# Three more entries get their products with Wa and adj ahead of their turn

## The chip, the cores and the metric

The kernel runs on one core of a Trainium2 chip. The metric is device time in microseconds, as the median of several runs; smaller is better. Five engines work side by side, each on its own list of instructions and in that list's order: PE (TensorE, products of matrices; its weight loads are shown apart as PEld), DVE (VectorE), ACT (ScalarE), POOL (GpSimd, which here issues the gathers and scatters) and SP (SyncE, which issues most plain transfers). They wait for each other by semaphores.

## The reference

32 entries of 512 nodes with 256 features go through four layers. Layers 0 and 3 are the same computation with other weights, cut here to what matters:

```python
pre_u = h @ W1[:d];  pre_v = h @ W1[d:]
S   = sigmoid(relu(pre_u[u] + pre_v[v] + b1) @ W2 + b2)     # for every pair (u, v)
a_t = (S * adj).T @ h
m_t = (adj.T @ h) * h
z   = beta1 * h + beta2 * (a_t @ Wa + ba) + beta3 * (m_t @ Wm + bm)
```

`adj` is 512 x 512 and mostly zero, so S is needed only where adj is not. Layer 1 is `z + relu((adj @ z) @ W.T + b)`. Layer 2 is an attention: a softmax over `leaky_relu(f1[i] + f1[j]) + adj`, applied to features.

Of layer 0, two parts need neither S nor any edge: `h @ Wa` (the kernel multiplies with Wa first, then with S) and `(adj.T @ h) * h`.

## The kernel before, in words

The kernel counts the entries of adj and takes a sparse path when they fit. There the 32 entries are worked off in eight groups of four (NB = 4); the time in which a group passes its middle stage is called a turn. For each group there are five streams of work, Python generators that issue a piece of work each time they are asked:

- `first` (L806): loads x of an entry, transposes it to hT, writes hT to memory as xT, and forms pre_u and pre_v, which SP writes to a table in memory (L604). Its products are L578 (transposes), L592 and L594.
- `edges` for layer 0: for each of 36 items (rows of nonzeros of adj) POOL gathers 128 rows of the table (L646), DVE adds the other side's rows (L731) and takes relu and W2 (L739 with sums on ACT at L717, or L747 with sums of its own), sigmoids follow (L614 to L675), and POOL scatters the results to cells (L639).
- `middle`: loads the cells as SA (L772), and for each of the four entries (`middle_one`, L876) ends layer 0, does layers 1 and 2, and forms pre_u and pre_v of layer 3.
- `edges` for layer 3, as above.
- `last` (L1094): ends layer 3 in the way the middle stage ends layer 0; its products with S are L1061.

In `middle_one` the order on PE is: mhT = (adj.T @ h) * h (`mhT`, L794, products at L46, DVE at L801); the product of hWa with S as laid out in `flat` (L891, ACT at L860); mhT with Wm (L898); layer 1 with zW (L912) and adjT (L46 with adjT); layer 2 with the features (L934), a transpose of their last column f (L950), a softmax on ACT and DVE (L958 to L964), the put-back of its rows by transposes (L1003, ACT at L1004), the product with eT (L46), then pre_u and pre_v (L592, L594) and transposes of the result (L992). hWa of the next entry (`hWa`, L782, products at L46 with Wa, ACT at L791) is made between the put-backs. z is formed in the tile of hT: ACT scales hT by beta1 (L896) and DVE adds the sums (L899). So each entry loads hT anew (L871, tile `hT1`, one buffer), and x into `h1` (L867) where it has to make mhT.

The first group is different: `middle_before` (L824) makes hWa and mhT of its four entries before the first turn begins, into four `big` tiles, which share their buffers (tag SA3, four of them) with the SA tiles of layer 3. The middle stage then uses these (`given`) and loads no x.

The order is written out by `weave` (L454). Each piece of each stream has a time, in units of a turn; all pieces are sorted by it. The first turn's middle stage goes from 0 to 0.53, the second's from 0.53 to 1.53, and so on. Within a stage `middle_shares` divides the time among the pieces by estimated costs, and the pieces of the edges fall between the pieces of the middle stage by these times. A stream with a list of costs (`first`, `last`) is fill: a due piece is held until a piece of the middle stage tells of room on PE (its yield's value: 0.9 after the features, 7.0 and 3.4 in the softmax, some 1.7 elsewhere) and is then issued behind that piece's last PE instruction. The framework's scheduler may bring an instruction forward in its engine's list where its inputs and its tile allow; `behind` and `issue_after` bar it from going ahead of the middle stage.

In the first turn no fill is due: the first stages of groups 0 and 1 are done before it, the first stage of group 2 is due from 0.71 to 0.97, and the last stage of group 0 from 1.09 to 1.69.

Of the kernel before, what the change touches and what calls it, by code (L numbers as in the profile page):

```python
# [8 lines left out]
F32 = mybir.dt.float32  # L9
# [7 lines left out]
P = 128  # L17
N = 512
D = 256
NC = N // P  # L20
DC = D // P
G = 32
NB = 4
# [25 lines left out]
class Model:  # L49


    def __init__(self, ctx, tc, a):
        nc = self.nc = tc.nc
        self.tc, self.a = tc, a
        const = self.const = ctx.enter_context(tc.tile_pool(name="const", bufs=1))
        self.ident = const.tile([P, P], F32, name="ident")
        make_identity(nc, self.ident)
        self.adj = const.tile([P, NC, N], F32, name="adj")
        for c in range(NC):
            nc.sync.dma_start(self.adj[:, c, :], a["adj"][c * P : (c + 1) * P, :])  # L60
        self.g0, self.g3 = self.gnn_first("L0_gnn"), self.gnn_first("L3_gnn")
# [361 lines left out]
class Sparse:  # L423
# [3 lines left out]
    def __init__(self, ctx, m, counts, xr, outr, B):  # L427
        self.m, self.nc, self.tc, self.counts = m, m.nc, m.tc, counts
        tc = m.tc
        self.xr, self.outr = xr, outr  # L430
        pool = lambda n, b, **k: ctx.enter_context(tc.tile_pool(name=n, bufs=b, **k))
        self.dram = pool("dram", 1, space=bass.MemoryType.DRAM)

        self.cells = {
            k: [self.dram.tile([CELLS + SPARE, NB], F32, name=f"cells_{k}{q}") for q in range(2)] for k in "03"
        }
        self.lists = self.dram.tile([N, 2 * N], F32, name="lists")
        self.x2s = self.dram.tile([B, P, NC, D], F32, name="x2s")

        self.xT, self.x2T = (self.dram.tile([B, P, DC, N], F32, name=n) for n in ("xT", "x2T"))  # L440
        self.e = Edges(m, pool("edges", 1))
        self.adjT = pool("adjT1", 1).tile([P, NC, N], F32, name="adjT")
        self.grp = pool("grp", 2)
        self.act, self.small, self.gath = pool("act", 1), pool("small", 2), pool("gath", 5)
        self.ps = pool("ps", 7, space=PSUM)
        self.ps_f1 = pool("ps_f1", 1, space=PSUM)
        self.later, self.bigs, self.given, self.marks = None, 0, None, {}
        self.main = None
        self.before = {(k, q): [] for k in "03" for q in range(2)}

# [352 lines left out]

    def first(self, g, i):  # L806


        def load(b):
            h = self.act.tile([P, NC, D], F32, name="h0", tag="h", bufs=2)  # L810
            self.nc.sync.dma_start(h, self.xr[i + b])
            return h

        h = load(0)
        for b in range(NB):
            ahead = load(b + 1) if b < NB - 1 else None
            hT = self.turned(h, "hT0", "hT")
            yield
            self.nc.scalar.dma_start(self.xT[i + b], hT)
            yield from self.pre(g, b, hT)  # L820
            h = ahead
        self.settle()

    def middle_before(self, g0, i):  # L824

        self.given = []
        for b in range(NB):
            h, hT = self.fresh(i + b)
            hT = hT()
            both = self.big(F32, 2048, 3).rearrange("p (k n) -> p k n", k=2)  # L830
            hWa = both[:, 0, :].rearrange("p (c d) -> p c d", c=NC)
            mhT = both[:, 1, :].rearrange("p (c n) -> p c n", c=DC)
            for _ in self.hWa(g0, hT, 0, hWa):
                yield
            for _ in self.mhT(h, hT, 0, mhT):
                yield
            self.given.append((hWa, mhT))

    def middle(self, g0, g3, i):


        SA = self.load(g0, 0)
        given, self.given = self.given, None
        h, hT = self.fresh(i, given)
        hT = hT()
        hWa = None
        if not given:
            for hWa in self.hWa(g0, hT, 0):
                yield
        flat = self.flat(SA, 0)  # L850
        for b in range(NB):
            keep = [h, hT, hWa, flat]
            yield from self.middle_one(g0, g3, b, i + b, SA, keep, given)
            h, hT, hWa, flat = keep
        self.settle()
# [20 lines left out]
    def middle_one(self, g0, g3, b, i, SA, keep, given):  # L876
        nc, m, w = self.nc, self.m, g0.w
        act, small, psum = self.act, self.small, self.psum
        h, hT, hWa, flat = keep
        if given:  # L880
            hWa, mhT = given[b]
        else:
            for mhT in self.mhT(h, hT, 0):
                yield
# [15 lines left out]
            yield 4.0 * (c == DC - 1)  # L900
        more = b < NB - 1
        if more:
            keep[0], turned = self.fresh(i + 1, given)

        zW = act.tile([P, NC, D], F32, name="zW", tag="hWa0")
        halves = [(0, psum()), (2, psum())]
# [20 lines left out]
        eT = act.tile([P, NC, N], F32, name="eT")  # L927
        if more:
            keep[1] = turned()
            ahead = None if given else self.hWa(g0, keep[1], 0)  # L930
        pns = [psum() for _ in range(NC)]
        for r in range(DC):
            for ic, pn in enumerate(pns):
# [4 lines left out]
                    start=(r == 0),  # L938
# [182 lines left out]
def even(n):  # L1121
    return [1.0] * n
# [2 lines left out]

FIRST, LAST, AHEAD = even(NB * 5 + 1), even(NB * 8 + 1), even(NB * 4 + 1)
ENDS, BEHIND = even(NB * 6 + 1), even(NB * 2 + 1)


def spread(shares, a, b):  # L1130

    times, at = [], 0.0
    for share in shares:
        times.append(a + (b - a) * at / sum(shares))
        at += share
    return times
# [6 lines left out]
    return first + spread(even(ITEMS), a, b) + spread(even(TAIL), b, behind)  # L1143


def middle_shares(given):


    hWa = [] if given else [1.7, 1.7]
    shares = list(hWa)  # L1150
    for b in range(NB):
        more = hWa if b < NB - 1 else []
        shares += [] if given else [2.8, 2.8]
        shares += [3.4, 3.4, 1.0, 2.7]
        shares += [1.7, 3.4, 2.8, 4.5] + [0.9] * NC
        shares += [0.4, 0.4, 0.4, 1.0, 0.4, 1.0] + more + [1.5, 1.5]
        shares += [2.8, 4.5] + [0.4] * NC + [0.5, 0.5]
    return shares + [0.1]


@with_exitstack
def sparse_path(ctx, m, counts, xr, outr, B):


    sp = Sparse(ctx, m, counts, xr, outr, B)
    last = B // NB - 1
    streams = [
        (sp.setup(), spread(even(NC + 1 + NC + 2 * (OWN // 2 + 1) + 1), -0.40, -0.295), ""),
        (sp.setup_behind(), spread(even(2 * (OWN // 2 + 1) + 2 * PANELS + 4), -0.285, -0.16), ""),
        (sp.setup_rest(), spread(even(7), -0.26, -0.20), ""),  # L1170
        (sp.zeros_behind(), spread(even(2), 0.15, 0.2), ""),
    ]
    for t in range(last + 1):
        g0, g3 = Group(sp, m.g0, f"0_{t}"), Group(sp, m.g3, f"3_{t}")
        start, end = (max(0.0, k - 0.47) for k in (t, t + 1))

        if t == 0:
            first = spread(FIRST, -0.385, -0.30)
            edges0 = edge_times(-0.292, -0.27, -0.03, -0.02, LEAD_AT_ENDS)
        elif t == 1:  # L1180
            first = spread(FIRST, -0.28, -0.06)
            edges0 = edge_times(0.02, 0.07, start - 0.06, start - 0.04)
        else:
            first = spread(FIRST, start - 0.82, start - 0.56)
            edges0 = edge_times(start - 0.552, start - 0.505, start - 0.06, start - 0.04)
        edges3 = edge_times(end + 0.003, end + 0.05, end + 0.48, end + 0.54)
        behind = end + 0.56, end + 1.16
        if t == last - 1:
            edges3 = edge_times(end + 0.003, end + 0.05, end + 0.46, end + 0.5)
            behind = end + 0.7, end + 1.06  # L1190
        if t == last:
            end -= 0.2
            edges3 = edge_times(end + 0.003, end + 0.02, end + 0.45, end + 0.46, LEAD_AT_ENDS)
            behind = end + 0.29, end + 0.45
        streams += [
            (sp.first(g0, t * NB), first, FIRST_US),
            (sp.edges(g0, ("yT", "mhT0", "hWa0") if t == 0 else ()), edges0, ""),
            (sp.middle(g0, g3, t * NB), spread(middle_shares(t == 0), start, end), "main"),
            (
                sp.edges(g3, *((("yT", "h1", "hT1"), ("mhT0", "hWa0")) if t == last else ())),  # L1200
                edges3,
                "free",
            ),
        ]
        if t == 0:
            streams.append((sp.middle_before(g0, 0), spread(AHEAD, -0.15, -0.03), ""))
        if t < last:
            streams.append((sp.last(g3, t * NB), spread(LAST, *behind), LAST_US))
        else:
            streams.append((sp.last_before(g3, t * NB), spread(ENDS, *behind), ""))  # L1210
            streams.append((sp.last_behind(g3, t * NB), spread(BEHIND, end + 0.5, end + 0.6), ""))
    sp.weave(streams)
# [237 lines left out]
```

## Time and profile before

| what | value |
|---|---|
| median of 3 runs | 2996.85 us |
| the runs | 2991.82 to 2997.82 us |
| the profiled execution | 2998.45 us |
| its span | 2996.8 us |
| busy: PE, DVE, POOL, ACT | 90%, 77%, 52%, 45% |
| setup, first stages, first edges | 0 to 245 us |
| first turn (four entries given) | 245 to 475 us |
| second turn | 475 to 814 us |
| third turn | 814 to 1155 us |

In a line of a timeline the columns are start, length, engine, line, operation, tiles written and read, shape, count, and in brackets how long the engine had been idle and what ended that. A line of a table of windows has the window, its length, the busy time of PE, PEld, DVE, ACT and POOL (with the number of instructions), the granted clock of PE, the share of the DMA engines and GB/s. A product of 512 columns takes about 0.43 us of PE at full clock (16 of them pass in 6.87), though the mean of one is given as 592 ns, since they overlap.

### The profile page before, as it was taken

The numbers are of one execution on the slowest core, as the hardware profiler recorded it, in microseconds if no ns is written. First come the engines' busy times: TensorE is split into PE (matmuls) and PEld (weight loads), VectorE is DVE, ScalarE is ACT, GpSimd is POOL, SyncE is SP. The second block draws the span as 40 slices with busy tenths as digits, with TensorE's granted clock in tenths as the row PEclk, the third lists the DMA queues.
The fourth block names the chain that finished last, engine by engine and source line by source line (L and its number), as shares of the span: only waits on it lengthen the run. The fifth ranks groups of instructions, "written<-read, shape, count | busy, mean of one in ns | idle before, by whom it ended". The sixth has DMA issues, their size and how long they took to land. (4 is left out here: it accounts for less than half of the span.)

```text
span 2996.8 us, 32453 instructions
## 1 busy us (share of the span) xinstructions
PE 2690.0 (90%) x8645; PEld 1613.9 (54%) x8646; DVE 2307.1 (77%) x6035; ACT 1336.8 (45%) x4101; POOL 1555.3 (52%) x1328
## 2 busy tenths in 40 slices
PE   6367787989998999989999899989999899988998
PEld 3134344545664566546664466646565466644666
DVE  6874786889588885988778885888858896783494
ACT  3553454445344443544344443445434453453262
POOL 2662463646445673556536464466735564361183
PEclk9678998999999999999999999999999999999999
DMA  8875657796678867787677866687677866663474
GB/s 268 286 225 169 213 174 221 233 300 203 217 217 269 268 211 227 230 262 254 209 222 247 275 207 230 216 268 253 211 228 236 303 227 197 208 211 102 148 244 150
DMA packets 302143, 677.30 MB, mean 226 GB/s; under 512 B 52608, under 2 KB 170880, under 8 KB 293760
## 3 DMA queue, kind: packets, MB, share of 16 engines
q0 software_dynamic: 122688, 414.40, 42.9%
q1 hardware_dynamic: 160304, 223.52, 23.0%
q10 hardware_dynamic: 18960, 37.24, 3.4%
q8 instruction: 70, 1.15, 0.2%
q14 instruction: 121, 0.99, 0.1%
HBM read 529.02 MB, written 146.01 MB: 225 GB/s over the span
## 5 line engine op out<-in xcount | busy, mean ns | idle before, releaser
L646 POOL DMA_INDIRECT rows<-table,iv x552 | 679.0, 1230 | 795.5 <-DMA table<-puv 262.7
L639 POOL DMA_INDIRECT cells<-s,cell x576 | 697.6, 1211 | 420.6 <-DVE s L675 243.2
L731 DVE TENSOR_TENSOR rows<-rows,mine 128x1024 f32<-128x1024 f32 x552 | 666.4, 1215 | 101.4 <-DMA rows<-table,iv 72.8
L717 ACT ACTIVATE rows<-rows 128x256 f32<-128x256 f32 x1088 | 439.6, 406 | 445.4 <-DVE rows L739 396.6
L46 PE MATMUL pst<-adj,h 128*128 128x512 f32 x1024 | 452.2, 592 | 0.0
L747 DVE SCALAR_TENSOR_TENSOR rows<-rows,L_gnn_W2bc 128x256 f32<-128x256 f32 x1120 | 414.0, 417 | 1.6
L739 DVE SCALAR_TENSOR_TENSOR rows<-rows,L_gnn_W2bc 128x1024 f32<-128x1024 f32 x272 | 329.4, 1213 | 0.4
L46 PEld LDWEIGHTS pst<-adj,h 128*128 128x128 f32 x1024 | 192.8, 190 | 219.9 <-issue 217.6
L46 PE MATMUL pst<-L_gnn_Wa,hT 128*128 128x256 f32 x1024 | 248.8, 393 | 62.9 <-DMA hT<-xT 57.8
L46 PEld LDWEIGHTS pst<-L_gnn_Wa,hT 128*128 128x128 f32 x1024 | 198.9, 199 | 103.0 <-issue 59.2
L46 PE MATMUL pst<-eT,feats 128*128 128x512 f32 x512 | 237.7, 619 | 10.9 <-ACT eT L1004 10.9
L46 PE MATMUL pst<-adjT,zW 128*128 128x512 f32 x512 | 228.2, 599 | 11.6 <-ACT zW L916 9.7
L596 DVE TENSOR_TENSOR puv<-pst,bc_L_gnn_b 128x256 f32<-128x256 f32 x256 | 104.9, 416 | 162.4 <-DMA table<-puv 89.2
L597 ACT COPY puv<-pst 128x256 f32<-128x256 f32 x256 | 93.2, 371 | 288.1 <-DVE puv L596 225.9
L1061 PE MATMUL pst<-hWa,SA 128*128 128x256 f32 x896 | 220.3, 400 | 0.0
L1061 PEld LDWEIGHTS pst<-hWa,SA 128*128 128x128 f32 x896 | 213.8, 328 | 3.7 <-issue 1.7
L717 ACT ACTIVATION_READ_ACCUMULATOR rows<-rows 128x1 f32 x1088 | 204.7, 188 | 0.0
L860 ACT COPY flat<-SA 128x512 f32<-128x512 f32 x128 | 136.7, 1128 | 136.6 <-issue 62.9
L891 PE MATMUL pst<-flat,hWa 128*128 128x512 f32 x448 | 196.8, 592 | 0.0
L592 PE MATMUL pst<-w_L_gnn_W,hT 128*128 128x512 f32 x256 | 141.5, 681 | 53.9 <-ACT hT L579 36.5
L46 PEld LDWEIGHTS pst<-eT,feats 128*128 128x128 f32 x512 | 99.9, 198 | 133.2 <-issue 113.3
L46 PEld LDWEIGHTS pst<-adjT,zW 128*128 128x128 f32 x512 | 96.5, 191 | 133.4 <-issue 114.0
(176 smaller groups left out, 3984.2 us busy)
## 6 DMA issues: line engine op xcount, KB each, us to landing
table<-puv SPq DMA_DIRECT2D x256, 256.0 KB
SA<-cells POOLq DMA_DIRECT2D x64, 1024.0 KB
h<-in_x_dram SPq DMA_DIRECT2D x64, 512.0 KB
mine<-table SPq DMA_DIRECT2D x64, 512.0 KB
hT<-xT SPq DMA_DIRECT2D x36, 512.0 KB
xT<-hT ACTq DMA_DIRECT2D x32, 512.0 KB
x2T<-yT SPq DMA_DIRECT2D x32, 512.0 KB
x2s<-x ACTq DMA_DIRECT2D x64, 256.0 KB
```

Source lines behind the costliest of these rows:

```text
L46: nc.tensor.matmul(out, lhsT, rhs, start=(n == 0), stop=(n == len(pairs) - 1))
L592: nc.tensor.matmul(pp, hT[:, 0, ks], w["W1"][:, 0::DC, :], start=True, stop=False)
L596: nc.vector.tensor_tensor(puv[:, 0, :], pp[:, 0:D], w["b1bc"], ALU.add)
L639: ins = self.nc.gpsimd.indirect_dma_start(out=g.cells[half], out_offset=bass.IndirectOffsetOnAxis(ap=at, axis=0), in_=s, in_offset=None)
L646: self.nc.gpsimd.indirect_dma_start(out=rows, out_offset=None, in_=g.table, in_offset=bass.IndirectOffsetOnAxis(ap=at, axis=0))
L717: self.behind(nc.scalar.activation(part, part, AF.Identity, accum_out=g.s[:, k, b : b + 1]))
L731: self.behind(nc.vector.tensor_tensor(rows, rows, other, ALU.add))
L739: nc.vector.scalar_tensor_tensor(by_entry, by_entry, 0.0, w2, ALU.max, ALU.mult)
L747: nc.vector.scalar_tensor_tensor(part, part, 0.0, w["W2bc"], ALU.max, ALU.mult, accum_out=at)
L860: self.nc.scalar.copy(flat[:, r, :], SA[r][:, :, b])
L891: nc.tensor.matmul(pz, hWa[:, r, cs], flat[:, r, :], start=(r == 0), stop=False)
L1061: self.nc.tensor.matmul(pz[:, k * D : (k + 1) * D], SA[r][:, cs, b], hWa[:, r, :], start=(r + k == 0), stop=(alone and k == 1 and r == NC ...
```

## The change

The second group's entries 0, 1 and 2 are made as the first group's are, by `middle_before`, now with a number of entries `n`. It runs as fill during the first turn: its four pieces for an entry (two halves of hWa, two of mhT) are due at 1.5, 2.5 and 3.5 entries into the first turn, at stated costs of 1.7, 1.7, 3.4 and 3.4, and the end of the generator at 4.5. Each takes the `big` tile that the first turn's entry 0, 1 or 2 has left. Here it loads x into the tile tag `h` and hT into the tag `hT`, which are those of `first` and `last`, and not into `h1` and `hT1` of the middle stage. The middle stage of the second turn uses what is given for entries 0 to 2, and makes hWa and mhT for entry 3 as before. `given` becomes a list for each group, and `middle_shares` divides a turn by the number of entries that are given.

```diff
-    def middle_before(self, g0, i):
+    def x_of(self, i):
+        h = self.act.tile([P, NC, D], F32, name="h0", tag="h", bufs=2)
+        self.nc.sync.dma_start(h, self.xr[i])
+        return h
...
+    def middle_before(self, g0, i, n=NB):
-        self.given = []
-        for b in range(NB):
-            h, hT = self.fresh(i + b)
-            hT = hT()
+        given = self.given[i] = []
+        for b in range(n):
+            if i:
+                h = self.x_of(i + b)
+                hT = self.act.tile([P, DC, N], F32, name="hT0", tag="hT")
+                self.nc.sync.dma_start(hT, self.xT[i + b])
+            else:
+                h, hT = self.fresh(i + b)
+                hT = hT()
...
-        given, self.given = self.given, None
+        given = self.given.pop(i, [])
...
-        if given:
+        if b < len(given):
             hWa, mhT = given[b]
...
-            keep[0], turned = self.fresh(i + 1, given)
+            keep[0], turned = self.fresh(i + 1, b + 1 < len(given))
...
-            ahead = None if given else self.hWa(g0, keep[1], 0)
+            ahead = None if b + 1 < len(given) else self.hWa(g0, keep[1], 0)
...
+GIVEN = {0: NB, 1: NB - 1}
+AHEAD_US = [1.7, 1.7, 3.4, 3.4]
...
+def ahead_times(end):
+    entry = end / NB
+    return [(k // 4 + 1.5) * entry for k in range(4 * GIVEN[1] + 1)]
...
-    hWa = [] if given else [1.7, 1.7]
-    shares = list(hWa)
+    hWa = [1.7, 1.7]
+    shares = [] if given else list(hWa)
     for b in range(NB):
-        more = hWa if b < NB - 1 else []
-        shares += [] if given else [2.8, 2.8]
+        more = hWa if given <= b + 1 < NB else []
+        shares += [] if b < given else [2.8, 2.8]
...
-            (sp.middle(g0, g3, t * NB), spread(middle_shares(t == 0), start, end), "main"),
+            (sp.middle(g0, g3, t * NB), spread(middle_shares(GIVEN.get(t, 0)), start, end), "main"),
...
+        if t == 1:
+            streams.append((sp.middle_before(g0, NB, GIVEN[1]), ahead_times(start), AHEAD_US))
```

More of the change, by code (lines that the diff above doesn't have):

```diff
@@ L446, in __init__ @@
         self.ps_f1 = pool("ps_f1", 1, space=PSUM)
-        self.later, self.bigs, self.given, self.marks = None, 0, None, {}
+        self.later, self.bigs, self.given, self.marks = None, 0, {}, {}
         self.main = None
@@ L802, in mhT @@
             yield mhT
+    def x_of(self, i):
+        h = self.act.tile([P, NC, D], F32, name="h0", tag="h", bufs=2)
+        self.nc.sync.dma_start(h, self.xr[i])
+        return h
     def first(self, g, i):
[L809 to L814, printed above, removed]
+        h = self.x_of(i)
         for b in range(NB):
-            ahead = load(b + 1) if b < NB - 1 else None
+            ahead = self.x_of(i + b + 1) if b < NB - 1 else None
             hT = self.turned(h, "hT0", "hT")
@@ L836, in middle_before @@
                 yield
-            self.given.append((hWa, mhT))
+            given.append((hWa, mhT))
     def middle(self, g0, g3, i):
         SA = self.load(g0, 0)
-        given, self.given = self.given, None
+        given = self.given.pop(i, [])
         h, hT = self.fresh(i, given)
```

## The prediction

> **What bounds the kernel now.** I read the shares of the engines first, then the span by stage, then PE in the first turn, and last the waits of the engines that stand beside it. The page's first part says that PE is the busiest engine over the span and DVE the next:
>
> ```profile
> PE 2690.0 (90%) x8645; PEld 1613.9 (54%) x8646; DVE 2307.1 (77%) x6035; ACT 1336.8 (45%) x4101; POOL 1555.3 (52%) x1328
> ```
>
> An average says nothing about a change that touches two of eight turns, so the next view is the busy time of each engine by entry. The first four rows are the four entries of the first turn (245 to 475 us), then a row for each entry of the second, and the last is the whole third turn. Columns: window, its length, PE, PEld, DVE, ACT, POOL, granted clock, DMA share, GB/s.
>
> ```profile
> 245.20:303.80 58.60, 48.01 (x133) 25.11 (x132) 30.00 (x74) 25.89 (x56) 6.45 (x6) 0.88 0.44 143
> 303.80:365.40 61.60, 44.52 (x134) 23.55 (x133) 45.39 (x116) 30.05 (x87) 33.04 (x32) 0.89 0.67 218
> 365.40:422.50 57.10, 47.29 (x134) 24.53 (x133) 46.22 (x120) 30.10 (x87) 31.77 (x26) 0.88 0.57 182
> 422.50:474.90 52.40, 45.79 (x135) 24.39 (x134) 34.98 (x109) 23.46 (x57) 20.62 (x20) 0.90 0.49 172
> 474.90:551.50 76.60, 65.05 (x204) 36.48 (x203) 64.48 (x168) 37.46 (x113) 40.21 (x34) 0.93 0.77 233
> 551.50:644.30 92.80, 81.00 (x240) 42.37 (x239) 79.96 (x242) 43.52 (x130) 53.78 (x44) 0.94 0.78 254
> 644.30:726.40 82.10, 77.03 (x262) 48.11 (x261) 72.18 (x181) 40.75 (x129) 53.43 (x45) 1.00 0.79 253
> 726.40:813.90 87.50, 85.78 (x286) 54.42 (x285) 61.09 (x169) 32.55 (x94) 45.28 (x39) 1.00 0.62 206
> 813.90:1155.00 341.10, 324.92 (x1060) 195.18 (x1059) 279.56 (x757) 154.06 (x462) 191.52 (x160) 0.99 0.74 239
> ```
>
> See three things. In the first turn PE is idle 44 us of 230 and the granted clock is low; nothing is full there, and the entry's own chain sets the pace. In the first two entries of the second turn PE and DVE are both near 85%, so neither alone is the bound. In its last entry PE is at 98%.
>
> Where PE is idle in the first turn stands in the timeline of PE. One softmax (transpose of f at L950, then the put-backs at L1003):
>
> ```profile
> 391.06 0.95 PE L950 MATMUL f<-ident,feats 128*128 128x128 f32 x4
> 398.28 1.09 PE L1003 MATMUL pst<-ident,ex 128*128 128x128 f32 x4 [6.28 <-DVE cols L963]
> 399.78 1.12 PE L1003 MATMUL pst<-ident,ex 128*128 128x128 f32 x4 [0.41 <-DVE ex L964]
> 401.99 1.12 PE L1003 MATMUL pst<-ident,ex 128*128 128x128 f32 x4 [1.09 <-DVE ex L964]
> 403.40 1.12 PE L1003 MATMUL pst<-ident,ex 128*128 128x128 f32 x4 [0.30 <-DVE ex L964]
> 405.25 9.71 PE L46 MATMUL pst<-eT,feats 128*128 128x512 f32 x16 [0.73 <-ACT eT L1004]
> ```
>
> And what starts the second turn: the 16 products with Wa and the 16 with adj, end to end, ahead of the first product with S (L891):
>
> ```profile
> 474.90 3.62 PE L46 MATMUL pst<-L_gnn_Wa,hT 128*128 128x256 f32 x16
> 478.35 7.03 PE L46 MATMUL pst<-adj,h 128*128 128x512 f32 x16
> 485.22 7.03 PE L891 MATMUL pst<-flat,hWa 128*128 128x512 f32 x16
> ```
>
> **The change part by part.** The sum is made against the profiled execution, 2998.45 us (span 2996.8 and 1.65 around it), which is 1.6 above the median 2996.85.
>
> *What moves.* Per entry 3.45 us of PE for hWa (474.90 to 478.35) and 6.87 for mhT (478.35 to 485.22): 10.3, and for three entries 30.9. With each go two ACT copies (0.58) and two DVE products (0.69). They leave the second turn (all 10.3 of the start; 10.3 each between the starts of entries 0 and 1 and of entries 1 and 2) and come into the softmaxes of entries 1, 2 and 3 of the first: the due time 1.5 entries lies just before that entry's feats, so the first half of hWa goes into the room of 0.9 ahead of f's transposes and the other three pieces into the room of 7.0 behind them.
>
> *First turn, what it costs.* The windows from f to the product with eT:
>
> ```profile
> 330.93:350.74 19.81, 5.12 (x21) 3.27 (x20) 15.19 (x42) 11.38 (x29) 9.97 (x9) 0.66 0.52 167
> 391.06:405.25 14.19, 5.27 (x21) 3.27 (x19) 12.19 (x35) 11.30 (x29) 6.44 (x7) 0.70 0.47 152
> 447.52:458.75 11.23, 5.17 (x21) 3.27 (x19) 7.38 (x21) 8.10 (x18) 4.91 (x7) 0.67 0.73 276
> ```
>
> In each, PE needs at least 10.3 of fill, 0.95 for f, 1.8 for the four put-backs at their quick spacing (4 x 0.44, as at 792 us) and about 1 for the last copy: 14.1. The chain itself grows by the 1.7 of the piece ahead of f, and by up to 2.5 if both DVE products and both copies fall into it. Entry 1: 19.81 covers the fill, so +2.5. Entry 2: 14.19 + 1.7, so +1.7. Entry 3: the fill is longer than the chain, 14.1 - 11.2 = +2.9. Together +7.1. Against it: the 16 products with eT took 9.71 and 8.56 behind the idle gaps of entries 2 and 3, and 7.13 in entry 1, where put-backs ran close before; with PE kept busy I take back 2.6 + 1.4 = 4.0. That leaves +3. Bounds: 30.9 if nothing is hidden, -4 if all is and the quicker products stay.
>
> [...]
>
> *Loads.* Each of the three entries loads x and xT on SP. The x loads take no new place: SP's list shows loads of x for the third turn (line L811) issued at 117.54 and 168.38 as soon as a tile was free, some 350 us ahead of their use at 524.64, and the moved entries take those places. The third turn's then wait for tiles freed at some 345, 400 and 460, still ahead of 524. New are three loads of hT (0.33 us of SP and 512 KB each; the middle stage loads hT again, since it becomes z in place). The first is issued when the first stage leaves its tile, near 220, just ahead of the loads at 227.33 and 228.06 on which PE waits 6.00 us at 233.29: +1 (0 to 3, at 1 MB in some 6 us). The other two come at about 345 and 400 behind the products before them; SP waits there with table writes and `mine` loads behind it, and SP stood 27 us at 246.14 in this trace with no engine waiting for what lay behind. 0, and up to 3 if the cover is gone. POOL: the four SA loads for layer 3 now need tiles that entries 0 to 2 of the second turn release; before, they went out from 641.18 to 659.73 and were used at 690.61. The last now waits for entry 2's product with Wm (L898, 658 before, some 635 after), behind it on POOL stand gathers. 0, up to 3.
>
> *Second turn, what it gives.* Start and entry 0 together lose 20.6 of PE, but edges of layer 3 can't start earlier: POOL's first gather waits for the last table write and goes at 481.74, rows are there at some 487. From 485.2 to 558.4, the next entry's first product, DVE is busy 65.7 of 73.2. DVE's 68.2 from 474.9 on falls by 1.4 (two products) and by 6.5: with fewer shares per entry the plan gives this one 15.7 items of edges for 18.1, each 2.7 (1.22 + 1.21, or 1.22 + 4 x 0.36, and a share of the sigmoids). Of the 60.3 left, 3.9 lie ahead of 487; 56.4 end at 543 if DVE never waits, at 550 at its 90% of before. Entry 1 starts then, not at 558.4: a gain of 9 to 15, I take 12. In entry 1 (558.4 to 651.2) PE falls from 81.0 by 10.3 and gains the 5.2 of the first stage's fill (L578, L592, L594) that no longer fits entry 0's softmax: 76 of PE, and some 75 of DVE. At 87%, as before, that is 87 us; at the 94% of entry 2, 81; I take 8 of gain (5 to 10.3). Entry 2 keeps its work. Entry 3 gets 3.9 more items of edges, 10.5 of DVE on 61 of 87.5: 1.5 back (0 to 5). Sum -18.5.
>
> *A new wait.* With mhT given, nothing but the load of hT holds ACT's scaling (L896), and it can stand in front of the softmax. That is seen in the first turn, where all four entries were given:
>
> ```profile
> 336.49 0.81 ACT L896 ACTIVATE hT<-hT,L_gnn_bcol,bc_L_gnn_beta 128x512 f32<-128x512 f32 x1 [4.99 <-DMA hT<-xT]
> 337.20 2.40 ACT L958 ACTIVATE ex<-f,fcol 128x512 f32<-128x512 f32 x4
> ```
>
> Queued behind it: the four `ex` of the softmax, and DVE and PE behind those. In the first turn's three softmaxes the gaps were about 0, 4.99 and 0.96; three more entries at that mean of 2.0 make 6, half of it covered by other work: +3 (0 to 15). [...] The row at 395.42 with 0.96 says that the load is mostly there.
>
> Sum: +3 + 1 - 18.5 + 3 = -11.5, 2987 for the profiled execution, **2985 for the median**.
>
> **The rivals.** (B) *DVE takes the bound over in the second turn.* For it: 90% in entry 0. Against it: 61 us of idle DVE in the turn. Entry 0 gives 9, entry 1 5, entry 3 takes 5, the wait on hT 6; with +4 in the first turn the change is +1 (2990 to 3002 with its bounds; 2998).
> (C) *Slower: the fill stands in front of the put-backs in PE's order and is not hidden.* Place: the three softmaxes of the first turn. Price: up to 30.9; at +26, entries 2 and 3 fully exposed and half of entry 1, the sum is 26 + 1 - 15.5 = +11.5, 3008. It decides from a cost of 20.5, where the sum passes +6. For it: the chain of entry 3 is 11.2 long and the fill 10.3, so that little disorder exposes it. Against it: 8 to 15 us of idle PE in each window, and data loaded long before.
> (D) *All of the 30.9 comes out.* First turn +1, second -30.9 + 3 for the wait: -27, 2970. Against it: the gathers that start at 481.74 whatever PE does.
> (E) *The change does nothing:* the pieces slip out of the first turn because the room is not found. They would land in the second turn, as before: 2997. The rooms of 0.9 and 7.0 in each entry speak against it.
>
> **How the numbers follow.** Two times that differ by under 0.2% (6 us) can't be told apart here: the three runs of before span 6.0. Forecast 0.48 (2975 to 2991, its own range), D 0.13, B 0.17, E 0.03, C 0.19. Faster: D, the forecast but for 0.02, and a small part of B's lower end, 0.60. Slower: C and B's end above 3003, 0.20. The rest, 0.20, is the same. The range of 8 in 10 goes from D's middle to part of C: 2968 to 3004.
>
> **What would show it.** Right: products with Wa and adj writing `big` inside 330 to 475, three runs of 16 of each; the window of entry 3 from f to eT near 14 us, entries of the first turn longer by 3 us at most, eT's 16 products near 7.1; the second turn opening with L891 and no L46 with Wa; its entries 0 and 1 some 20 us shorter together; DVE in entry 0 above 90%. Wrong: PE idle before a product that writes `big` with a DMA of hT as its releaser (C, by the loads); L1003 waiting on nothing but PE (C); ACT L896 idle for more than 5 us on hT<-xT in the second turn; later turns of another length than 341, which nothing here foresees and which would make the sum wrong by what the order of instructions alone does.

## The result and the profile after

| what | before | after |
|---|---|---|
| median | 2997.82 us | 3016.02 us |
| the runs | 2991.82 to 2999.68 us | 3010.5 to 3025.14 us |
| ratio, 95% interval | 1 | 1.007 (1.0045 to 1.0095) |
| the profiled execution | 2998.45 us | 3025.14 us (span 3023.5) |

The changed kernel is slower by 18 us where 12 us of gain were forecast; the time lies 12 us above the upper end of the range. A second comparison is among the experiments (ratio 1.0062). The profiled execution is the slowest of the five, 9 us above their median; where a second profiled execution of the same kernel (3000.2 us, from that comparison) shows something else, it stands beside the first.

Lines below the diff stand some five further down in the changed kernel: L891 is now L896, L896 is L901, L899 is L904, L950 is L955, L964 is L969 and L1003 is L1008.

The page's first part, the busy time of the engines over the span, of the kernel after:

```profile
PE 2701.3 (89%) x8645; PEld 1622.4 (54%) x8646; DVE 2308.1 (76%) x6035; ACT 1335.6 (44%) x4101; POOL 1558.4 (52%) x1328
```

The work of these engines is the same to the instruction and PE's share has fallen: 27 us of span came, of which PE is busy for 11, at a lower granted clock (0.953 for 0.959 over the span), and DVE, ACT and POOL for 3.1 or less. Where they came stands in the busy time by entry, with the same marks as in the prediction (four entries of the first turn, four of the second; window, length, PE, PEld, DVE, ACT, POOL, granted clock, DMA share, GB/s), of the kernel after:

```profile
241.80:300.90 59.10, 47.44 (x133) 25.58 (x132) 30.02 (x74) 25.73 (x56) 6.44 (x6) 0.88 0.44 140
300.90:365.20 64.30, 55.92 (x166) 29.95 (x165) 46.63 (x118) 30.98 (x89) 33.94 (x32) 0.92 0.70 229
365.20:426.60 61.40, 55.47 (x167) 29.92 (x166) 47.36 (x122) 30.79 (x89) 31.11 (x26) 0.92 0.56 182
426.60:479.80 53.20, 51.83 (x167) 28.63 (x166) 35.95 (x111) 25.78 (x61) 20.40 (x20) 1.00 0.50 179
479.80:553.90 74.10, 53.82 (x149) 28.19 (x148) 55.58 (x144) 32.89 (x99) 33.27 (x28) 0.82 0.71 214
553.90:644.80 90.90, 74.64 (x217) 38.68 (x216) 77.68 (x232) 43.35 (x136) 50.88 (x42) 0.92 0.72 233
644.80:732.30 87.50, 72.02 (x231) 45.29 (x230) 69.46 (x185) 35.91 (x115) 56.38 (x48) 0.90 0.77 246
732.30:833.10 100.80, 91.11 (x294) 56.92 (x293) 70.92 (x194) 36.30 (x107) 50.20 (x43) 0.97 0.61 198
```

| stage | before, us | after, us | difference | after, second execution | difference |
|---|---|---|---|---|---|
| first turn, entry 0 (no fill) | 58.6 | 59.1 | +0.5 | 57.8 | -0.8 |
| first turn, entries 1 to 3 | 171.1 | 178.9 | +7.8 | 179.7 | +8.6 |
| second turn, entries 0 and 1 | 169.4 | 165.0 | -4.4 | 161.6 | -7.8 |
| second turn, entries 2 and 3 | 169.6 | 188.3 | +18.7 | 182.0 | +12.4 |

The first turn began 3.4 us earlier than before (241.8 for 245.2). At the start of the third turn 19.2 us are lost, at that of the fourth 23.0 (its first product with S comes at 1191.78 for 1168.80), at the end 26.7. In the second execution 8.2 are lost at the start of the third turn and 1.7 at the end. So the 8 us of the first turn and the pattern of the second (its first half shorter, its second half longer by more) are in both; some 10 of the second turn's 14.3, and what was lost behind it, are not.

In the second turn PE's busy time fell from 308.9 to 291.6 us, and its granted clock from 0.97 to 0.91. In entry 2 PE is now busy 72 of 87.5 us; before, 77 of 82. The time came as idle time. This is what ended PE's waits there, the waits of PE over the second turn (engine, tile and line that waited, what it waited for; us in total, times, longest), of the kernel after:

```profile
PE pst L1008 <- DVE ex L969: 25.6, 8, 10.5
PE f L955 <- ACT feats L947: 7.0, 2, 6.8
PE pst L917 <- issue: 6.0, 1, 6.0
PE pst L46 <- ACT eT L1009: 5.3, 3, 2.8
```

and the head of the same view of the kernel before:

```profile
PE pst L1003 <- DVE ex L964: 8.7, 3, 7.3
PE pst L592 <- ACT hT L579: 4.5, 1, 4.5
```

The put-backs of the softmax wait 25.6 us for the DVE step before them (8.7 before): the gap that the products and the first stage's fill used to cover is open, and the step at its end comes no earlier. In the second execution they wait 22.0.

In the first turn the fill went where it was to go. PE's timeline for the softmax of its entry 2 (start, length, engine, line, operation, tiles, shape, count, idle time before and its releaser), of the kernel after:

```profile
389.73 1.89 PE L46 MATMUL pst<-L_gnn_Wa,hT 128*128 128x256 f32 x8
391.45 0.60 PE L955 MATMUL f<-ident,feats 128*128 128x128 f32 x4
391.89 1.89 PE L46 MATMUL pst<-L_gnn_Wa,hT 128*128 128x256 f32 x8
393.62 7.03 PE L46 MATMUL pst<-adj,h 128*128 128x512 f32 x16
400.48 0.60 PE L1008 MATMUL pst<-ident,ex 128*128 128x128 f32 x4
...
406.13 1.12 PE L1008 MATMUL pst<-ident,ex 128*128 128x128 f32 x4 [2.89 <-DVE ex L969]
...
409.80 9.22 PE L46 MATMUL pst<-eT,feats 128*128 128x512 f32 x16 [1.05 <-ACT eT L1009]
```

The fill runs in the gap, with no wait for a load, and ends when the first put-back is ready. But the 16 products with eT still take 9.22 us and not 7.13. The three windows from f to eT and, last, the stretch of the put-backs alone, of the kernel after:

```profile
329.67:348.47 18.80, 12.72 (x45) 7.31 (x44) 16.80 (x44) 11.75 (x29) 10.05 (x9) 0.84 0.66 209
391.45:409.80 18.35, 12.50 (x46) 7.12 (x44) 12.79 (x32) 11.53 (x29) 4.78 (x5) 0.84 0.45 152
453.29:465.07 11.78, 10.95 (x46) 6.62 (x44) 8.16 (x22) 9.87 (x20) 3.32 (x5) 1.00 0.73 290
400.50:409.80 9.30, 3.45 (x18) 2.20 (x17) 8.45 (x21) 5.33 (x17) 0.89 (x1) 0.68 0.35 113
```

Only in entry 3 does the clock stay at 1.00. In entry 2 it is 1.00 in the fill behind f (391.89 to 400.50) and 0.68 in the 9.3 us behind it, where PE is idle 5.85 us in pieces.

Entry 2's window grew most, by 4.2 us. What it waited for shows in ACT's timeline at its start, of the kernel before:

```profile
392.04 2.42 ACT L958 ACTIVATE ex<-f,fcol 128x512 f32<-128x512 f32 x4 [0.41 <-PE f L950]
395.42 0.81 ACT L896 ACTIVATE hT<-hT,L_gnn_bcol,bc_L_gnn_beta 128x512 f32<-128x512 f32 x1 [0.96 <-DMA hT<-xT]
```

and of the kernel after:

```profile
394.25 0.81 ACT L901 ACTIVATE hT<-hT,L_gnn_bcol,bc_L_gnn_beta 128x512 f32<-128x512 f32 x1 [3.96 <-DMA hT<-xT]
...
395.44 1.84 ACT L963 ACTIVATE ex<-f,fcol 128x512 f32<-128x512 f32 x3
```

ACT's scaling of the next entry's hT now stands ahead of the softmax and waits for its load, and the first `ex` starts 4.0 us behind f, for 1.0 before. All five traces with the fill have this order and a wait of 3.6 to 4.2 us there; before it was 0.96.

The wait that the prediction added to the second turn is there, twice: 3.56 us in the softmax of entry 0 (at 516.26) and 5.04 in entry 1. In entry 1, ACT's timeline of the kernel after:

```profile
595.83 0.81 ACT L901 ACTIVATE hT<-hT,L_gnn_bcol,bc_L_gnn_beta 128x512 f32<-128x512 f32 x1 [5.04 <-DMA hT<-xT]
...
598.15 0.89 ACT L947 COPY feats<-pst 128x257 f32<-128x257 f32 x3
```

The copies of the features stand behind it, and f behind them (the 6.8 in PE's waits above).

### The profile page after: what moved, and what is told of

The parts are those of the page before. It is cut to its first block, busy times and chain, and to the rows that moved or that the text cites. A ratio compares the mean times of both kernels' runs of the same rounds, so it can differ in the third digit from the quotient of the medians.

```text
span 3023.5 us, 32446 instructions
## 1 busy us (share of the span) xinstructions
PE 2701.3 (89%) x8645; PEld 1622.4 (54%) x8646; DVE 2308.1 (76%) x6035; ACT 1335.6 (44%) x4101; POOL 1558.4 (52%) x1328
## 5 line engine op out<-in xcount | busy, mean ns | idle before, releaser
L731 DVE TENSOR_TENSOR rows<-rows,mine 128x1024 f32<-128x1024 f32 x552 | 666.5, 1216 | 115.5 <-DMA rows<-table,iv 75.7
L596 DVE TENSOR_TENSOR puv<-pst,bc_L_gnn_b 128x256 f32<-128x256 f32 x256 | 104.8, 416 | 158.0 <-DMA table<-puv 73.9
L896 PE MATMUL pst<-flat,hWa 128*128 128x512 f32 x400 | 175.7, 592 | 0.0
```

Source lines behind the costliest of these rows:

```text
L596: nc.vector.tensor_tensor(puv[:, 0, :], pp[:, 0:D], w["b1bc"], ALU.add)
L731: self.behind(nc.vector.tensor_tensor(rows, rows, other, ALU.add))
L896: nc.tensor.matmul(pz, hWa[:, r, cs], flat[:, r, :], start=(r == 0), stop=False)
```

## The experiments

Three theories were stated with the first runs; their letters are not those of the prediction's rivals. **A**: the second turn is paced by DVE or by the order of the edges' instructions among the middle stage's, the products were covered there and their leaving gains nothing. **B**: the times that `middle_shares` gives to the pieces that remain do the harm, not the products. **C**: the fill itself disturbs, by its loads or tiles. Each kernel is compared with the kernel before, run beside it on the same chip; "old times" are the times that the remaining pieces had in the kernel before, "new times" those of the changed kernel.

### The change in its parts

Fill alone: made in the first turn and then left unused, while the second turn forms its products as before at the old times.

```diff
-        given = self.given.pop(i, [])
+        given = self.given.pop(i, []) if i == 0 else []
```

> The three entries are made as fill in the first turn, but the second turn doesn't use them: it makes its own products, at the times of before. 30.9 us of PE more than before, so this is the price of the fill alone. Theory A (the second turn is paced by DVE and by the order of edges in front of its softmax, and loses its cover with the products): first turn +8 as in the changed kernel, the second as before, 3003 to 3008. Theory B (the new times of the pieces do the harm): the same, since the times are those of before. Theory C (the fill itself, its loads and tiles, disturbs what follows): 3015 or more.

Measured: 1.0025 (1.0008 to 1.0042), 2983.07 for 2974.66 us, +8.4. Its first turn has the same entries 1 to 3 as the changed kernel: from the first product with S at 295.42 to the start of the second turn at 474.70 they take 179.3 us (171.1 before). The fill costs 8 us, and all of it where it stands; of C that much holds.

The products taken out, with no fill; the second turn's entries 0 to 2 read the first group's tiles instead. New times first, then old times:

```diff
-            streams.append((sp.middle_before(g0, NB, GIVEN[1]), ahead_times(start), AHEAD_US))
...
-        given = self.given.pop(i, [])
+        given = self.given.get(0, [])[: GIVEN.get(i // NB, 0)]
```

> No fill; in the second turn entries 0 to 2 use the products that the first group left in the same tiles, so they compute with another group's hWa and mhT and the output is not the reference's. 30.9 us of PE less than before, times of the pieces as in the changed kernel. The forecast of before the result: 20 us faster, 2978. Theory A: no faster than before, 2997 to 3010. Theory B: slower, like the changed kernel, some 3005 to 3012. Theory C: 2978, since no fill is there.

> The products of entries 0 to 2 are left out of the second turn (another group's are used, so the output is not the reference's), no fill, times of before, and nothing else: 30.9 us of PE less in the second turn. The forecast before the result: 20 us faster. Theory A (the chain of the middle stage through DVE, with the edges' instructions in between, sets the pace, and PE only waits longer): within 8 of before.

Measured: 1.0015 (0.9996 to 1.0035), 2981.71 for 2974.66, with new times; 1.0011 (0.9994 to 1.0027), 2986.94 for 2983.05, with old times. **30.9 us of PE work less, nothing put in its place, and no gain at all.**

The changed kernel with old times, and the kernel before with new times and nothing moved:

```diff
-            (sp.middle(g0, g3, t * NB), spread(middle_shares(GIVEN.get(t, 0)), start, end), "main"),
+            (sp.middle(g0, g3, t * NB), middle_times(there, counted, start, end), "main"),
...
+def middle_times(there, counted, start, end):
...
+    times = spread([x if c else 0.0 for x, _, c in full], start, end)
+    return [t for t, (_, k, _) in zip(times, full) if k]
```

(`full` has all pieces of a turn; a piece of an entry below `counted` gets no share of the time, one of an entry below `there` isn't issued.)

> The changed kernel, but in the second turn each piece that is left has the time that it had before the change, so that edges and fill fall between the same pieces as before. Theory B: the loss goes, 2980 to 2995. Theory A: it stays, 3008 to 3020, since PE still has less to do in front of each softmax and DVE as much. Theory C: it stays.

> The kernel before, with no product moved, but in the second turn the times of the changed kernel: the pieces that the change takes away are still there and count nothing in the plan. Theory B: slower by 10 to 20, 3007 to 3017. Theories A and C: within 6 of before, 2991 to 3003.

Measured: 1.0044 (1.0028 to 1.006), 2985.68, +11; and 1.0053 (1.0035 to 1.0071), 2988.23, +14. So new times do harm with nothing else changed, and B is a part of it but not the whole: with old times the changed kernel is still slower. The parts add up within their intervals: fill +8, taking out +4, together the +11 of the changed kernel at old times. What is left to its 1.0062 to 1.007, some 6 us, is put down to the new times by subtraction; the intervals overlap (1.0028 to 1.006 and 1.0042 to 1.0082), so this share is not shown by itself.

The changed kernel again, beside some of these:

> The changed kernel once more, beside these on one chip: 1.007 of before, as measured, 1.005 to 1.009.

Measured: 1.0062 (1.0042 to 1.0082), 3008.55 for 2991.89.

### Why less work gains nothing

The two edge streams of the second turn made empty, in the kernel before and with the products taken out:

```diff
+        if g.name in ("3_0", "0_2"):
+            for _ in range(LEAD + ITEMS + TAIL):
+                yield
+            return
```

> The kernel before, but the two streams of edges that fall into the second turn do nothing: no gathers, no DVE work, no scatters of theirs (the cells keep what an earlier group left, so the output is not the reference's). Every theory: faster, since DVE, POOL and the transfers are relieved; PE's own work is some 300 us of the turn's 339, so 20 to 40 us faster.

> The same without the two streams of edges, and without the products of entries 0 to 2 in the second turn. To be read against the run before it. Theory A: with no edges between the steps of the chain PE is the bound, and the 30.9 come out nearly whole, 20 to 31 us faster than that run. If something other than the edges holds the turn (the load of hT, the chain of the softmax alone): under 12.

Measured: 0.9931 (0.9906 to 0.9956), 2957.6 us, and 0.9826 (0.9797 to 0.9854), 2927.85 us. Without the edges, the same removal that gave nothing gives 29.75 us of the 30.9. The windows from one entry's f to the next (from the last f of the first turn; columns as above) show it entry by entry. Products taken out at old times, edges there:

```profile
445.00:509.00 64.00, 45.97 (x134) 25.26 (x133) 38.94 (x103) 26.66 (x72) 19.68 (x20) 0.87 0.70 227
509.00:590.00 81.00, 66.62 (x196) 35.93 (x195) 74.07 (x203) 43.39 (x138) 52.52 (x44) 0.89 0.75 239
590.00:692.00 102.00, 77.04 (x218) 42.45 (x217) 80.92 (x236) 40.94 (x128) 55.41 (x49) 0.85 0.82 260
```

The kernel before without the edges:

```profile
443.00:503.50 60.50, 54.48 (x167) 29.88 (x166) 17.64 (x45) 21.23 (x39) 5.46 (x7) 0.94 0.35 124
503.50:582.50 79.00, 73.57 (x228) 40.53 (x227) 28.00 (x78) 27.44 (x54) 0.00 (x0) 0.96 0.32 108
582.50:661.30 78.80, 77.84 (x248) 44.25 (x247) 28.60 (x81) 25.51 (x50) 0.00 (x0) 1.00 0.28 96
```

The same with the products taken out:

```profile
448.00:498.00 50.00, 43.40 (x134) 24.01 (x133) 16.25 (x43) 19.91 (x37) 5.38 (x8) 0.93 0.45 159
498.00:567.00 69.00, 62.95 (x197) 34.46 (x196) 26.35 (x76) 27.45 (x54) 0.54 (x1) 0.95 0.39 132
567.00:638.50 71.50, 69.46 (x215) 38.67 (x214) 27.32 (x79) 22.76 (x46) 0.54 (x1) 0.98 0.34 113
```

Without edges each stretch loses some 10 us. With them, the kernel before has 65.1, 89.7 and 92.0 in these three stretches (447.52, 512.63, 602.30 and 694.34 in its trace), together 246.8; with the products taken out they are 64.0, 81.0 and 101.8, together 246.8 as well. The stretch from entry 0's f to entry 1's gave 8.7 and the next took 9.8. The other three traces with the products gone at old times show the same two (79.2 to 82.4, then 99.6 to 101.3).

What holds the sum where it was is seen by counting one step of the edges, DVE's add of the other side's rows (L731), in DVE's timeline from the last f of the first turn on. The table gives us from that f to the add of that number (72 in the turn, 36 for each of the two layers):

| add | before | products out, old times | changed, old times | changed kernel | changed kernel, second execution | products out, new times | before, new times |
|---|---|---|---|---|---|---|---|
| 1st | 40.1 | 38.4 | 39.0 | 39.4 | 38.8 | 38.5 | 45.6 |
| 18th | 96.8 | 96.3 | 96.2 | 106.3 | 105.6 | 105.3 | 111.1 |
| 36th | 184.0 | 182.7 | 184.1 | 197.1 | 194.8 | 192.6 | 194.4 |
| 54th | 261.3 | 261.1 | 261.0 | 266.3 | 262.4 | 261.4 | 265.4 |
| 71st | 326.8 | 323.4 | 325.8 | 351.1 | 340.1 | 338.7 | 342.1 |
| 72nd | 337.9 | 334.4 | 336.9 | 354.9 | 345.0 | 342.5 | 345.9 |

With old times the edges run through the second turn at the same pace, to within 4 us in 338, whether PE has its 30.9 us of products there or not; 4 us is also what executions differ by, since the run with the fill alone, whose second turn is that of before, has 333.7 for the 72nd. Between the edges stand the steps of the middle stage, in written order. That the stage therefore goes at the edges' pace is a reading of this table, which the runs without edges support. With new times the edges fall behind in the first entries (the plan gives these fewer items), by 8 to 14 us at the 18th, and the last is still 5 to 17 late. How late does not tell what each version loses: the kernel before with new times lost 14, the changed kernel some 6 by them, and with the products out and no fill the new times cost nothing that can be told (1.0015 for 1.0011).

What DVE itself waits for in the long entry (589.9 to 691.7), the head of DVE's waits with the products taken out at old times:

```profile
DVE puv L596 <- DMA table<-puv: 12.8, 3, 6.8
DVE s L618 <- ACT s L614: 4.3, 1, 4.3
```

and in the same entry of the kernel before (602.3 to 694.3):

```profile
DVE puv L596 <- issue: 4.9, 1, 4.9
DVE puv L596 <- DMA table<-puv: 4.2, 1, 4.2
```

DVE is busy 81 of 102 us, so it is not full either: it stands at L596, which needs a tile that a table write has to free, with edges and stage steps behind it in its list. Of its three waits 5.2 us lie in the first stage and the longest, 6.8, in the middle stage's own pre_u.

The same in the changed kernel, in DVE's timeline between the products with Wm (which end on PE at 655.2) and the add that layer 1 of entry 2 needs:

```profile
655.43 1.23 DVE L731 TENSOR_TENSOR rows<-rows,mine 128x1024 f32<-128x1024 f32 x1 [1.04 <-DMA rows<-table,iv]
...
656.67 1.23 DVE L731 TENSOR_TENSOR rows<-rows,mine 128x1024 f32<-128x1024 f32 x1
...
659.27 1.22 DVE L739 SCALAR_TENSOR_TENSOR rows<-rows,L_gnn_W2bc 128x1024 f32<-128x1024 f32 x1
660.41 1.27 DVE L904 TENSOR_TENSOR hT<-hT,pst 128x512 f32<-128x512 f32 x2
```

The sum on PE is ready at 655.2; DVE takes it up at 660.41, behind two items of edges. That is PE's 6.0 us in front of L917 in its waits.

Is it the supply of the gathers? Every second gather of the two streams left out, the rows of the one before used twice:

```diff
+            if g.name in ("3_0", "0_2") and n % 2:
+                fetched[n] = self.even, t
+                return
```

> The kernel before, but in the second turn every second gather of rows is left out, and its item works on the rows of the item before (wrong sums, so the output is not the reference's); DVE and ACT do the same work as before. If the supply of gathered rows holds the edges and with them the turn: 8 to 20 us faster. If DVE's own work and its order do: within 8 of before.

Measured: 1.0004 (0.999 to 1.0017), 2981.33 for 2983.05. Half the gathers change nothing; their supply does not set the pace.

Is it DVE's busy time? DVE's add of the edges left out in the second turn (72 x 1.2 us), in the kernel before, and with the products taken out at old times:

```diff
-            self.behind(nc.vector.tensor_tensor(rows, rows, other, ALU.add))
+            if not g.name in ("3_0", "0_2"):
+                self.behind(nc.vector.tensor_tensor(rows, rows, other, ALU.add))
```

> The kernel before, but the edges that fall into the second turn (layer 3 of the first group, layer 0 of the third) leave out the addition of the other side's rows on DVE (L731, 72 of them, 1.22 us each), so their S is wrong and the output is not the reference's. DVE's busy time in the turn falls from 278 to some 190 us. Theory A (DVE and the order on it set the pace there): 10 to 25 us faster than before. If PE sets the pace: 0 to 5 faster.

> The same leaving out, and the products of entries 0 to 2 are left out of the second turn as in the run that only took them away (another group's are used), at the times of before. To be read against the run before it, which differs by the 30.9 us of PE alone. Theory A: with DVE relieved the products' 30.9 come out at last, 15 to 28 us faster than that run. If the gathers or the scaling on ACT hold the turn: within 8 of it.

Measured: 1.0178 (1.0158 to 1.0199), 3043.05 for 2991.89, 51 us slower with 87 us of DVE work less, where a gain was expected; and 1.0058 (1.0035 to 1.008), 3012.61. DVE's waits in the second turn, of the kernel before without the adds:

```profile
DVE rows L748 <- DMA rows<-table,iv: 90.3, 31, 12.3
DVE rows L740 <- DMA rows<-table,iv: 38.5, 18, 7.8
```

DVE now waits 129 us for gathered rows, with the stage's steps behind these waits (12.2 us in the kernel before for gathered rows of either side, in 9 waits). The edit changed the order as well as the work, so it does not answer the question it was made for. It shows another thing: work taken from the busy engine of an ordered list cost more here than it saved. Against this slowed base the products do come out, at 30 us, with the gathers, the scatters and the rest of the edges' work still there. So it is not the mere presence of edges that takes the gain; DVE's adds, or the order of its list with them in it, are part of it.

### The new wait, and two moves in the plan

ACT's scaling of hT held behind what stands before it in the written order, with the products taken out, and in the changed kernel, both at old times:

```diff
-            nc.scalar.activation(zT[:, c, :], hT[:, c, :], AF.Identity, bias=w["bcol"][:, c, :], scale=w["beta1"])
+            last = self.last_of(nc.scalar.engine)
+            ins = nc.scalar.activation(
+                zT[:, c, :], hT[:, c, :], AF.Identity, bias=w["bcol"][:, c, :], scale=w["beta1"]
+            )
+            if i // NB == 1:
+                order = mybir.DependencyInfo(mybir.DependencyClass.NoSync, mybir.DependencyReason.DATA)
+                self.tc.add_manual_dep(ins.ins, last, order, reason="not ahead of the softmax")
```

> The products of entries 0 to 2 are left out of the second turn (another group's are used, so the output is not the reference's), no fill, times of before, and ACT's scaling of hT (L896 of before) may not go ahead of the ACT instruction that stands before it in the program, so that it can't stand in the softmax and wait for its load. If that wait took the gain: 10 us or more faster than before. Theory A: within 6 of before.

> The changed kernel with the times of before in the second turn, and ACT's scaling of hT held behind the ACT instruction that stands before it in the program, in the second turn. Without the holding it was 1.0044. If the wait on hT is a cost of 3 to 6 us as in the run with products taken out (0.9991 against 1.0011): 1.002 to 1.0035. If it is none: 1.004 to 1.005.

Measured: 0.9991 (0.9979 to 1.0002), 2989.28 for 2991.89, against 1.0011 not held; and 1.0045 (1.0022 to 1.0067), 3008.01 for 2997.15, against 1.0044 not held. The runs not held are from other chips. The intervals overlap in the first pair and the second pair is equal. The wait on hT in the second turn is real and costs nothing that these runs can tell. The hold acts there alone; in entry 2 of the first turn ACT still waits 3.56 us.

The edge streams of the second turn 0.015 of a turn (some 5 us) later in the kernel before:

```diff
+            edges3 = edge_times(end + 0.003 + 0.015, end + 0.05 + 0.015, end + 0.48 + 0.015, end + 0.54 + 0.015)
...
+            edges0 = edge_times(start - 0.552 + 0.015, start - 0.505 + 0.015, start - 0.06 + 0.015, start - 0.04 + 0.015)
```

> The kernel before, with layer 3's edges of the first group and layer 0's of the third 0.015 of a turn later (5 us) and nothing else changed. If the place of the edges between the steps of the middle stage decides, as theory A has it: a change of 3 to 15 us, sign open. If only the amount of work does: within 3 of before.

Measured: 0.9987 (0.997 to 1.0004), 2994.75 for 2997.15. A shift as a whole costs nothing: its 18th add is 10.8 us late (107.6) and its last in time again (337.7 for 337.9). The new times cost 14 us, and there the last is 8 late. So it is not lateness in the plan alone but how the items are spread among the stage's pieces.

Other work for the first turn's gaps: the first stage of the third group due there (0.15 to 0.5) in the kernel before, with nothing else moved.

```diff
-            first = spread(FIRST, start - 0.82, start - 0.56)
+            first = spread(FIRST, start - 0.82, start - 0.56) if t > 2 else spread(FIRST, 0.15, 0.5)
```

> The kernel before, with the first stage of the third group (transposes, products with W1, their 16 x 3 DVE instructions, the table) due from 0.15 to 0.5 instead of 0.71 to 0.97: fill of 41 us of PE and some 20 us of DVE moved out of the second turn into the first. Theory A: the second turn gains what DVE loses and more, 10 to 20, the first costs 10 to 20, since each softmax there hides some 8 of 10; 0 to 10 faster in all. If PE's load alone counted: the second turn would gain 40.

Measured: 1.0031 (1.0012 to 1.0049), 3007.44 for 2997.15, +10. This does not pay either. No version that does the whole work was measurably faster than the kernel before.

## Why the prediction was wrong, by its own steps

- **What bounds the kernel.** It said of the second turn's first entries that PE and DVE are both near 85%, "so neither alone is the bound". That was a right reading of shares and stopped there: what sets the end is the stream of edges with the stage's steps between them, and it has idle time of its own. The count of the edges' adds would have shown that stream in the trace of before.
- **Second turn, -18.5: this step failed.** It took the edges' start as fixed (right: 40.1 and 39.4 us after the last f) and their pace as DVE's busy time at 90%, and let the stage go faster with fewer items and less PE work. Entry 0 came out 2.5 shorter for 12, entry 1 1.9 for 8, entry 2 5.4 longer for none, entry 3 13.3 longer for 1.5: +14.3. In the second execution it is 2.9 and 4.9 shorter, 4.8 and 7.5 longer: +4.6. At old times the removal alone costs +4 (-2 to +8), and without edges it gives 29.75. With the whole of the edges there nothing of the 30.9 comes out: the gain behind entry 0's f (8.7 at old times) was real and was given back an entry later. One reading in the sum was off without changing it: DVE's work ahead of 487 is 3.2, not 3.9.
- **The plan's new times.** "Later turns of another length than 341, which nothing here foresees" was as near as the prediction came. The forecast took the fewer items in entry 0 (15.7 for 18.1) as less DVE work there, a part of the 12 of gain. They were edges put off, and the edges are what sets the end. Measured: +14 with nothing moved, some +6 in the changed kernel by subtraction, nothing with the products out and no fill.
- **First turn, +3: right mechanism, wrong size.** Measured +7.8 in the windows and +8.4 alone. The cost of the fill, +7.1, was close: the windows from f to eT became longer by -1.0, +4.2 and +0.6, and 1.7 each goes ahead of f, +8.9 in all. Entry by entry that is +0.7, +5.9 and +2.3 for +2.5, +1.7 and +2.9, so the sum is near in part by luck: in entry 2 the scaling of hT went ahead of the softmax and held it by 3 us, a wait that the prediction priced in the second turn only. The 4.0 to be taken back from quicker products with eT were the mis-sized term: 9.16, 9.22 and 7.13 for 7.13, 9.71 and 8.56 is +0.1. The 8.56 of entry 3 belonged to one execution: in ten traces of other kernels here with nothing put into that gap they take 7.13.
- **Loads, +1.** No product of the fill waited for a load, and the fill alone leaves nothing beyond its windows: about 0 there, within its bounds.
- **The new wait, +3.** It came twice in the second turn, 3.56 and 5.04 us, where the text put it (in the softmax or in front of it), 8.6 together, where the upper bound of 15 is three times the 4.99 of one row. Holding it back there changed nothing that could be told. The 5.04 is the text's own sign of being wrong, but not what made it wrong.
- **The rivals.** DVE's side as the bound (B) had the right mechanism with too small a price: it left entry 0 its gain of 9 and came to +1. The fill in front of the put-backs (C) was priced at 26 and is 8: its order was right, little was exposed. That all comes out (D) holds only where there are no edges. That nothing moves (E) is excluded by the timeline.

Open: which of DVE's work and the order of its list sets the edges' pace could not be told apart, since leaving out the adds changed both. Not tested is whether the table writes that L596 waits for (12.8 us in the long entry) set it. Also open is why spreading the items anew costs 14 us and a shift of the whole stream nothing.

## What to carry to other kernels

Where two streams are woven into the same in-order lists, find the one that sets the end by counting its steps against time in the trace; work taken from the other gave nothing here, and gaps that it left behind opened as waits. An entry that becomes shorter proves nothing until the same mark two entries later has moved too. When an edit also changes a planner's shares, price the new plan by itself, with nothing moved: here that alone cost 14 us.

## What the runs showed of the hardware that was not expected

Filling 8.6 us of PE's gap in entry 2 of the first turn (391.89 to 400.50, granted clock 1.00) did not keep the clock up: in the 9.3 us behind the fill, with PE idle for 5.85 us in pieces of 2.89 at most, the granted clock was 0.68 and the products with eT took 9.22 us instead of 7.13. Between the gaps stood short transposes, of 0.66 to 1.12 us for four. How much work in such a stretch would have kept the clock up no run here shows.

Taking 72 adds from DVE, 87 us of work, made the kernel 51 us slower: DVE then reached the gathered rows before they were there and waited 129 us for them.
